# Layer 0 of a two-layer block on one Trainium2 core: the mLSTM's column-group products of a block in one place, and the 64-feature chunk's low-rank and down products in one place

## The chip, the cores and the metric

The kernel runs on one core of one Trainium2 chip. A time is the device time of one execution in microseconds (us). The kernel before takes 770.57 us, the median of 3 runs (769.84 to 771.42). Everything is float32. TensorE is called PE here, VectorE DVE, ScalarE ACT, GpSimd POOL, and SyncE SP.

## The reference, cut to what matters

The input is 4 sequences of 512 tokens with 256 features. Two layers follow each other; each adds an attention-like part and a feed-forward part to the layer-normed input. The change touches two places of layer 0, the mLSTM's sums and the mixture of low-rank experts:

```python
# mLSTM, 8 heads, 16 key and 32 value features per head
C = (q @ k.T / sqrt(16)) * exp(Dmat - m)              # Dmat from the two gates
n = maximum(abs(C.sum(-1, keepdims=True)), exp(-m))
h = (C / n) @ v
# experts: 704 hidden features, 8 experts of rank 16, two of them chosen per token
base_out = (silu(gate_base) * up_base) @ Wd.T
for e in experts:
    h = silu(gate_base + g_lora_e) * (up_base + u_lora_e)
    acc += (h @ Ad_e.T @ Bd_e.T) * 2.0 * weight_e
x = x + mlstm_block(xn) + base_out + acc
```

The kernel computes the mLSTM block by block: 128 positions of all 4 sequences at a time, with a state (a 16x33 matrix per head and sequence) that goes from block to block.

## The kernel before

**Stages.** Layer 0 works through four blocks j of 128 positions x 4 sequences (512 tokens), layer 1 through the same four. In layer 0, `mlstm(j)` is the attention part, `experts(j)` the mixture, `mlp(j)` the second feed-forward part of the attention block; each is a Python generator that issues instructions.

**What sets the order.** Each engine runs its instructions in the order in which they were issued (`InOrder`). That order comes from a planner in the kernel's own Python: `Clock` keeps a guess of when each engine, tile and PSUM bank is free, and `Flow` always steps the generator that can go on first by that guess. `flow.wait(tiles, banks=n)` hands control away until the tiles are ready and n PSUM banks are free; `flow.add(gen, turn=...)` starts another stream, with a lower `turn` going first. So an edit in one place can move the instructions of all others.

**Array shapes.** A matmul whose operand has only 32 output columns or 32 or 64 contraction rows uses a part of PE's 128x128 array, and 4 or 2 of these run side by side. The profile writes the shape of the part as rows*columns. There are five kinds of such groups in layer 0, and everything else is 128*128:

- 32*128: the products `qk` (16 matmuls of 128 columns for each of two head parities) and `h_ps`, what the old state gives;
- 128*32: `hv` (values) and `sums` (denominators), 16 matmuls for each parity, and `st_ps`, the product for the new state, 16 matmuls of 66 columns;
- 128*64: the hidden chunk of 64 features of each half of the tokens ("pair"), up-projections and the two steps of low-rank corrections;
- 64*128: that pair's two products to the experts' ranks (`acc<-he_pair,lora`), and its four down products (`acc<-WdT,hid`, 64 rows).

**mlstm.** After the decays are known, the state's product is a stream of its own (`pass_on`): it transposes the keys to tokens, multiplies them with `wvs` into a PSUM tile `st_ps`, masks that on DVE and adds it to the decayed `state`. Meanwhile the main stream gets the decay matrices `ct[0]` and `ct[1]` (a DMA, a POOL select, a DVE subtraction and an ACT exponential each), multiplies them with `qk`, and then, for each parity s, issues `hv` and `sums` when `ct[s]` is ready.

**experts.** Of 704 hidden features, five chunks have 128 and the last 64. The order of work is the pair of 64-feature chunks, then five chunks of the first half of the tokens, then five of the second; each chunk has a base product and two low-rank steps, between which ACT and DVE read its bank (`gated`). Four turns later, its product to the ranks is added to `dps[half]`, a PSUM accumulator (`acc`). When the first half's five are through, the pair's product for both halves is added: it is the last one of `dps[0]` and the first of `dps[1]`. Then `finish(half, t)` scales `dps[half]` on DVE (`tmp<-acc,tmp`, then `dw<-tmp`), for half 0 at once; for half 1 it also issues the down products into two more accumulators `yps`: four of 64 rows, then for each half ten of `hid` and two of `dw` (`acc<-BdT,dw`), and DVE adds the result to x.

Of the kernel before, what the change touches and what calls it, by code (L numbers as in the profile page):

```python
# [13 lines left out]
P = 128  # L14
# [19 lines left out]
def layers_kernel(ctx: ExitStack, tc: tile.TileContext, io: dict, out: bass.AP):  # L34
# [168 lines left out]
    def mm_ps(name):  # L203
        count[0] += 1
        t = psum.tile([P, 512], F32, tag="mm", bufs=BANKS, name=f"{name}_{count[0]}")
        clock.take_bank(t)
        return t
# [20 lines left out]
    class Flow:  # L228
# [21 lines left out]
        def idle(self, t, why=""):  # L250
            if t > self.now:
                clock.stalls.append((self.now, t - self.now, "idle " + why))
                clock.free["pe"] = t

        def soon(self, us=0.5):
            return self.now + us
# [238 lines left out]
    with ExitStack() as l0:  # L495
# [5 lines left out]
        def tmp():  # L501
            return new(wk0, [P, 512], "tmp", 7)
# [199 lines left out]
        def mlstm(j):  # L702
# [149 lines left out]
            if not last:  # L852
                yield from flow.wait(dec)
                for b in range(B):
                    wvs.append(new(wk0, [P, H, DV + 1], "wv", 4))
                    pool.tensor_tensor(
                        out=wvs[b], in0=va[:, b, :, :], in1=spread_dec(new_n, b), op=ALU.mult)
            faded = set()

            def pass_on():  # L860

                k_tok = new(wk0, [P, B, P], "qs")
                yield from flow.wait(kT, banks=1)
                kt_ps = mm_ps("kt_ps")
                for b in range(B):
                    transpose(kt_ps[:, cols_of(b)], kT[:, cols_of(b)], ident)
                act.copy(k_tok, kt_ps.rearrange("p (b c) -> p b c", c=P))
                yield from flow.wait(*wvs, k_tok, banks=1)
                st_ps = mm_ps("st_ps")
                for b in range(B):  # L870
                    for r in range(H // 2):
                        mine = slice(32 * r, 32 * r + 32)
                        mm(st_ps[mine, b * W2 : (b + 1) * W2], k_tok[:, b, mine],
                           wvs[b][:, 2 * r : 2 * r + 2, :].rearrange("p i d -> p (i d)"),
                           start=True, stop=True, at_once=4)
                new_state = state if first else wvs[0].rearrange("p (b i) d -> p b i d", b=B)
                dve.tensor_tensor(
                    new_state, st_ps[:, 0 : B * W2].rearrange("p (b i d) -> p b i d", b=B, i=2),
                    parity.unsqueeze(1).unsqueeze(3).to_broadcast([P, B, 2, DV + 1]), ALU.mult)
                while not first and not faded:  # L880
                    yield flow.soon()
                if not first:
                    yield from flow.wait(state)
                    yield flow.spare()
                    dve.tensor_tensor(state, state, new_state, ALU.add)
                passed.add(j)

            if not last:
                flow.add(pass_on(), 1)
# [7 lines left out]
            if not first:  # L897
                for b in range(B):
                    mine = hr[:, b, :, :]
                    pool.tensor_tensor(out=mine, in0=mine, in1=spread_dec(old_n, b), op=ALU.mult)  # L900
                    yield flow.soon(0.6)
                if not last:
                    heads = state.rearrange("p b i d -> p (b i) d")
                    pool.tensor_tensor(
                        out=heads, in0=heads, in1=fade.rearrange("p b i -> p (b i)").unsqueeze(
                            2).to_broadcast([P, 2 * B, DV + 1]), op=ALU.mult)
                faded.add(j)
            for s in range(2):
                for r in range(0, H // 2, 2):
                    yield from flow.wait(ct[s])  # L910
# [8 lines left out]


            dve.tensor_copy(ones_at[:, :, DV], rr[:, 0, :])
            sums = None
            hvT = [ct[0][:, 2, :], ct[0][:, 3, :], ct[1][:, 0, 0:P]]

            def by_columns(out, lhsT, s, start, stop):
# [27 lines left out]
            for s in range(2):  # L953
                yield from flow.wait(ct[s], banks=4)
                qks = [mm_ps("qk") for _ in range(H // 2)]
                for b in range(B):
                    for r, qk in enumerate(qks):
                        mm(qk[:, cols_of(b)], kT[32 * r : 32 * r + 32, cols_of(b)],
                           qm[32 * r : 32 * r + 32, s, cols_of(b)], start=True, stop=True,
                           at_once=4)  # L960
                for r, qk in enumerate(qks):
                    dve.tensor_tensor(ct[s][:, r, :], qk, ct[s][:, r, :], ALU.mult)
            for s in range(2):
                yield from flow.wait(ct[s], banks=1 if sums else 2)
                hv = mm_ps("hv")
                by_columns(hv, lambda b, r: va[:, b, 2 * r + s, 0:DV], s, True, True)
                if not sums:
                    sums = mm_ps("sums")
                    clock.held.add(sums.tensor.name)
                by_columns(  # L970
                    sums[:, 0:P], lambda b, r: ones_at[:, b, DV - 2 * b - s : 2 * DV - 2 * b - s], s,
                    s == 0, s == 1)
                act.copy(hvT[s], hv)
                if s == 1:
                    act.copy(hvT[2], sums[:, 0:P])
                    clock.held.discard(sums.tensor.name)
            for n in range(3):
                yield from to_tokens(n)

# [166 lines left out]
        def experts(j):  # L1146
# [60 lines left out]
                while read[n] < 0:  # L1207
                    yield flow.soon(0.2)

            rooms, hb, he, dps = {}, {}, {}, {}  # L1210

            dws, mine = {}, [slice(half * (P // 2), (half + 1) * (P // 2)) for half in range(2)]

# [5 lines left out]
            def released(ps):  # L1219
                clock.held.discard(ps[:].tensor.name)  # L1220

            def finish(half, t):


                yield from flow.wait(dps[half])
                dve.tensor_tensor(t, dps[half], t, ALU.mult)
                dw = dws[half] = new(wk0, [P, T], "dw", 2)
                dve.tensor_tensor(dw, slots(t)[:, 0, :], slots(t)[:, 1, :], ALU.add)
                if half == 0:
                    return  # L1230
                yield from flow.wait(banks=2)
                yps = [acc() for _ in range(2)]

                def down(half, i, a, w, stop=False, **kw):
                    mm(yps[half][:, i * D : (i + 1) * D], a[:, i * P : (i + 1) * P], w, stop=stop,
                       skip_group_check=True, **{"start": False, **kw})

                for i in range(2):  # L1240
                    for half in range(2):
                        down(half, i, hb["pair"][mine[half], :], wdT[mine[half], last, :],
                             start=(i == 0), at_once=2)
                for half in range(2):
                    for i in range(2):
                        yield 0
                        for c in range(last):
                            down(half, i, hb[half, c], wdT[:, c, :])
                    yield from flow.wait(dws[half])
                    for i in range(2):  # L1250
                        down(half, i, dws[half], bdT, stop=(i == 1))
                    xv = xb[:, 2 * half : 2 * half + 2, :].rearrange("p b d -> p (b d)")
                    dve.scalar_tensor_tensor(xv, yps[half], 0.5, xv, ALU.mult, ALU.add)
                    released(yps[half])
                mixed.add(j)
# [23 lines left out]
            for i in range(len(order) + 4):  # L1279
# [33 lines left out]
                n = i - 4  # L1313
                if 0 < n < len(order):
                    _, half, c = order[n][0]
                    if (half, c) == (0, 0):
                        yield from flow.wait(banks=1)
                        dps[0] = acc()
                    yield from unread(n)
                    yield clock.ready(he[n])  # L1320
                    mm(dps[half], adT[:, c, :], he.pop(n), start=((half, c) == (0, 0)),
                       stop=((half, c) == (1, last - 1)))
                    if c < last - 1:
                        continue
                    if half == 0:

                        yield from unread(0)
                        yield from flow.wait(he[0], banks=1)
                        dps[1] = acc()
                        for h in range(2):  # L1330
                            mm(dps[h], adT[mine[h], last, :], he[0][mine[h], :], start=(h == 1),
                               stop=(h == 0), at_once=2)
                    weight = tmp()
                    for s in range(K_TOP):
                        dve.tensor_scalar(
                            slots(weight)[:, s, :], wT[:, here(half)],
                            (-LORA_SCALE, LORA_SCALE)[s], 0.0, ALU.mult, ALU.max)
                    if half == 1:
                        weighed.add(j)
                    released(dps[half])  # L1340
                    flow.add(finish(half, weight), turn=1)

        def main():
            for j in range(NJ):
# [271 lines left out]
```

## Time and profile before

| what | value |
|---|---|
| median of 3 runs | 770.57 us (769.84 to 771.42) |
| the profiled execution | 770.89 us |
| its span, first to last instruction | 769.1 us |
| PE matmuls busy in the span | 762.4 us (99%), 3792 records |
| PE weight loads busy | 518.2 us (67%) |
| DVE / ACT / POOL busy | 466.9 (61%) / 225.1 (29%) / 162.8 us (21%) |
| granted TensorE clock | 1.0 |

The profile's page has one line per group of like instructions, with the number, the mean duration of one and the idle time before it. All instructions of the recorded engines have line L221, the helper that issues them, so a group is told by its tiles: `acc<-he_pair,lora` writes tile `acc` and reads `he_pair` and `lora`. A float32 matmul is two records (passes) of PE; a transpose is one. Records of matmuls overlap, since they are pipelined: what one costs the next is the distance of their starts, not the duration. The timeline view lists merged instructions in order: start, length from the first start to the last end, engine, operation, tiles, array shape, form, number.

### The profile page before, as it was taken

The page shows a single profiled execution, that of the slowest core. Times are in us where ns is not written, and L with a number is a line of the kernel's source. Part 1 is how long each engine was busy: PE and PEld are TensorE (multiplying, and loading weights), DVE is VectorE, ACT ScalarE, POOL GpSimd, SP SyncE. Part 2 cuts the span into 40 slices and gives each one's busy share as a digit, 9 for nine tenths or more (in the row PEclk, how much of TensorE's full clock was granted, in tenths as well). Part 3 has the DMA queues.
Part 4 walks back from the last instruction along what each step waited for, and adds up shares of the span by engine and source line. Part 5 has one row for each costly group of instructions (what it writes and reads, how often), then busy time and mean ns, then how long its engine had stood idle before and what let it go on. Part 6 is the DMA issues. An engine that isn't in the chain of part 4 may idle for free.

```text
span 769.1 us, 9739 instructions
## 1 busy us (share of the span) xinstructions
PE 762.4 (99%) x3792; PEld 518.2 (67%) x3792; DVE 466.9 (61%) x1075; ACT 225.1 (29%) x457; POOL 162.8 (21%) x154
## 2 busy tenths in 40 slices
PE   9999999999999999999999999999999999999998
PEld 6786777766667875865777774747545664664487
DVE  6787576956544987633377635341376965934971
ACT  4334224332313343212133312010444224214300
POOL 6221051232041320240030041000333224013100
PEclk9999999999999999999999999999999999999999
DMA  7930000300000200000031110001000000000001
GB/s 236 291 109 1 2 1 0 97 15 0 2 1 1 111 0 1 2 1 0 1 111 36 75 43 13 1 0 55 0 1 0 1 27 1 0 29 0 1 14 42
DMA packets 18959, 25.44 MB, mean 33 GB/s; under 512 B 2784, under 2 KB 12768, under 8 KB 18912
## 3 DMA queue, kind: packets, MB, share of 16 engines
q1 hardware_dynamic: 17824, 24.53, 9.9%
q8 instruction: 30, 0.49, 0.3%
q10 hardware_dynamic: 1088, 0.28, 0.2%
q14 instruction: 17, 0.14, 0.1%
HBM read 22.65 MB, written 2.16 MB: 32 GB/s over the span
## 4 chain that ended last, share of the span: by engine, by line
PE 91%; DVE 8%; issue 1%; DMA 0%; POOL 0%; ACT 0%; SPq 0%; DVEq 0%; POOLq 0%
PE yp L221 18%; PE chunk L221 16%; PE up L221 14%; PE gp L221 14%; PE acc L221 10%; PE qk_ps L221 4%; PE pt L221 2%; PE vp L221 2%; PE o_ps L221 2%; PE v_ps L221 2%; PE lp L221 2%; DVE sl L221 1%; PE qk L221 1%; PE hv L221 1%; DVE tmp L221 1%; PE q_ps L221 1%
## 5 line engine op out<-in xcount | busy, mean ns | idle before, releaser
L221 PE MATMUL chunk<-low,lora 128*128 128x256 f32 (+1 forms) x384 | 86.3, 384 | 1.3 <-DVE he_pair L221 1.1
L221 ACT ACTIVATE sl<-chunk 128x256 f32<-128x256 f32 x132 | 50.7, 384 | 113.7 <-PE chunk L221 100.9
L221 PE MATMUL chunk<-xnT,wguT 128*128 128x256 f32 (+1 forms) x384 | 83.8, 383 | 0.0
L221 PEld LDWEIGHTS chunk<-xnT,wguT 128*128 128x128 f32 (+1 forms) x384 | 63.7, 181 | 20.5 <-issue 8.9
L221 PEld LDWEIGHTS chunk<-low,lora 128*128 128x128 f32 (+1 forms) x384 | 63.5, 181 | 17.1 <-issue 4.4
L221 DVE SCALAR_TENSOR_TENSOR sl<-sl,chunk 128x256 f32<-128x256 f32 x132 | 54.6, 414 | 23.9 <-ACT sl L221 23.5
L221 PE MATMUL up<-featT,w_up 128*128 128x512 f32 x128 | 60.4, 594 | 0.0
L221 PE MATMUL gp<-featT,w_gate 128*128 128x512 f32 x128 | 60.3, 593 | 0.0
L221 PE MATMUL up<-xnT,lora 128*128 128x512 f32 x128 | 60.2, 592 | 0.0
L221 PE MATMUL gp<-xnT,wguT 128*128 128x512 f32 x128 | 60.2, 592 | 0.0
L221 PE MATMUL yp<-w_down,hid 128*128 128x256 f32 x256 | 56.4, 379 | 0.0
L221 PE MATMUL yp<-w_gate,hs 128*128 128x256 f32 x256 | 56.1, 379 | 0.0
L221 PEld LDWEIGHTS yp<-w_down,hid 128*128 128x128 f32 x256 | 48.5, 190 | 8.2 <-issue 1.9
L221 PEld LDWEIGHTS yp<-w_gate,hs 128*128 128x128 f32 x256 | 48.6, 190 | 6.6
L221 DVE SCALAR_TENSOR_TENSOR tmp<-tmp,gp 128x512 f32<-128x512 f32 x32 | 22.0, 687 | 45.6 <-ACT tmp L221 45.6
L221 ACT ACTIVATE tmp<-gp 128x512 f32<-128x512 f32 x32 | 19.1, 597 | 95.0 <-PE gp L221 95.0
L221 POOL TENSOR_TENSOR pd<-k,q 128x256 f32<-128x256 f32 (+3 forms) x16 | 24.6, 1539 | 97.8 <-ACT k L221 96.5
L221 PEld LDWEIGHTS gp<-xnT,wguT 128*128 128x128 f32 x128 | 24.2, 190 | 28.8 <-issue 28.0
L221 PEld LDWEIGHTS up<-xnT,lora 128*128 128x128 f32 x128 | 24.2, 190 | 28.4 <-issue 27.5
L221 PEld LDWEIGHTS gp<-featT,w_gate 128*128 128x128 f32 x128 | 24.2, 190 | 28.1 <-issue 27.7
L221 PEld LDWEIGHTS up<-featT,w_up 128*128 128x128 f32 x128 | 23.9, 190 | 27.2 <-issue 26.1
L221 PE MATMUL acc<-tmp,lora 128*128 128x512 f32 x80 | 40.8, 598 | 0.0
(221 smaller groups left out, 1188.3 us busy)
## 6 DMA issues: line engine op xcount, KB each, us to landing
ct<-m_dram SPq DMA_DIRECT2D x8, 1024.0 KB, 8.5
x<-in_x SPq DMA_DIRECT2D x3, 512.0 KB, 9.7
out<-x SPq DMA_DIRECT2D x6, 256.0 KB, 2.2
w_gate<-in_w_gate SPq DMA_DIRECT2D x1, 1024.0 KB, 7.0
w_up<-in_w_up SPq DMA_DIRECT2D x1, 1024.0 KB, 7.6
w_down<-in_w_down SPq DMA_DIRECT2D x1, 1024.0 KB, 10.2
wguT<-in_f_gate SPq DMA_DIRECT2D x1, 1024.0 KB, 5.0
lora<-in_f_up SPq DMA_DIRECT2D x1, 1024.0 KB, 4.9
```

The source lines that it names most:

```text
L221: return tc.keep_in_program_order(f(*args, **kw))
```

## The change

It does three things. In `mlstm` the state's 16 products leave `pass_on`, which now only transposes the keys (its result goes into `k_toks`). The main stream waits for both `ct`, the weighted values, the keys and three free banks, and then issues both `hv`, both `sums` and the state's products one behind the other; the state's products go to columns 128 to 391 of the bank of `sums`. Between the groups it lets waiting streams with a negative turn go on (`flow.first`), which issue no matmuls. In `experts` the pair's product to the ranks moves from the middle of the block into `finish`, which is now one stream for both halves: it issues the two rank products and the four 64-row down products one behind the other, and a stream `low_rank` with turn -1 scales both `dps` on DVE after that; the products with `dw` wait for it. Both `dps` accumulators are held until then.

```diff
+        def first(self):
+            for s in [s for s in self.streams if s[2] < 0 and s[0] <= self.now]:
+                self.step(s)
...
                 act.copy(k_tok, kt_ps.rearrange("p (b c) -> p b c", c=P))
-                yield from flow.wait(*wvs, k_tok, banks=1)
-                st_ps = mm_ps("st_ps")
-                for b in range(B):
-                    for r in range(H // 2):
-                        mine = slice(32 * r, 32 * r + 32)
-                        mm(st_ps[mine, b * W2 : (b + 1) * W2], k_tok[:, b, mine],
...
-                passed.add(j)
+                k_toks.append(k_tok)
...
             for s in range(2):
-                yield from flow.wait(ct[s], banks=1 if sums else 2)
-                hv = mm_ps("hv")
-                by_columns(hv, lambda b, r: va[:, b, 2 * r + s, 0:DV], s, True, True)
-                if not sums:
-                    sums = mm_ps("sums")
-                by_columns(
...
+            while not last and not k_toks:
+                yield flow.soon()
+            yield from flow.wait(*ct, *([] if last else [*wvs, *k_toks]), banks=3)
+            hvs = [mm_ps("hv") for _ in range(2)]
+            sums = mm_ps("sums")
+            for s in range(2):
+                flow.first()
+                by_columns(hvs[s], lambda b, r: va[:, b, 2 * r + s, 0:DV], s, True, True)
+                flow.first()
                 by_columns(
                     sums[:, 0:P], lambda b, r: ones_at[:, b, DV - 2 * b - s : 2 * DV - 2 * b - s], s,
                     s == 0, s == 1)
+                act.copy(hvT[s], hvs[s])
+            if not last:
+                st = sums[:, P : P + B * W2]
+                for b in range(B):
+                    for r in range(H // 2):
+                        mine = slice(32 * r, 32 * r + 32)
+                        mm(st[mine, b * W2 : (b + 1) * W2], k_toks[0][:, b, mine],
...
+            act.copy(hvT[2], sums[:, 0:P])
+            if not last:
+                new_state = state if first else wvs[0].rearrange("p (b i) d -> p b i d", b=B)
+                dve.tensor_tensor(
...
+                if not first:
+                    dve.tensor_tensor(state, state, new_state, ALU.add)
+                passed.add(j)
...
-            def finish(half, t):
-                yield from flow.wait(dps[half])
-                dve.tensor_tensor(t, dps[half], t, ALU.mult)
-                dve.tensor_tensor(dw, slots(t)[:, 0, :], slots(t)[:, 1, :], ALU.add)
-                if half == 0:
-                    return
-                yield from flow.wait(banks=2)
+            def finish():
+                yield from unread(0)
+                yield from flow.wait(he[0], banks=2)
                 yps = [acc() for _ in range(2)]
+                for h in range(2):
+                    mm(dps[h], adT[mine[h], last, :], he[0][mine[h], :], start=False, stop=True,
+                       at_once=2, skip_group_check=True)
                 for i in range(2):
                     for half in range(2):
                         down(half, i, hb["pair"][mine[half], :], wdT[mine[half], last, :],
                              start=(i == 0), at_once=2)
+
+                def low_rank():
+                    for half, t in enumerate(weights):
+                        yield from flow.wait(dps[half])
+                        dve.tensor_tensor(t, dps[half], t, ALU.mult)
+                        released(dps[half])
+                        dve.tensor_tensor(dw, slots(t)[:, 0, :], slots(t)[:, 1, :], ALU.add)
+                flow.add(low_rank(), turn=-1)
...
-                    if half == 0:
-                        yield from flow.wait(he[0], banks=1)
-                        dps[1] = acc()
-                        for h in range(2):
-                            mm(dps[h], adT[mine[h], last, :], he[0][mine[h], :], start=(h == 1),
...
-                    flow.add(finish(half, weight), turn=1)
+            weighed.add(j)
+            flow.add(finish(), turn=1)
```

## The prediction

> **What bounds the kernel.** First the page: busy times, slices, and the chain that ended last.
>
> ```profile
> PE 762.4 (99%) x3792; PEld 518.2 (67%) x3792; DVE 466.9 (61%) x1075; ACT 225.1 (29%) x457; POOL 162.8 (21%) x154
> ...
> PEclk9999999999999999999999999999999999999999
> ...
> PE 91%; DVE 8%; issue 1%; DMA 0%; POOL 0%; ACT 0%; SPq 0%; DVEq 0%; POOLq 0%
> ```
>
> PE has work in 99% of the span at the full granted clock, and the chain is PE. So the time is the sum of the distances between starts of PE's records, plus its few waits, and an edit is worth what it does to these two. The number of records stays: the instruction order of the changed program has the same 2012 matmuls and transposes, and as many DVE, ACT and POOL instructions. What can change is what lies between the records, so I read PE's timeline in narrow windows. In the undisturbed stretches a pass of 512, 256 or 128 columns starts 429, 216 or 109 ns after the one before. Around the state's product and the pair's products of block 0 it doesn't:
>
> ```profile
> 36.63 0.38 PE L221 MATMUL chunk<-low,lora 128*128 128x256 f32 x1
> 36.94 0.67 PE L221 MATMUL st_ps<-wv,qs 128*32 128x66 f32 x32
> 37.54 0.70 PE L221 MATMUL chunk<-xnT,wguT 128*128 128x256 f32 x2
> ```
>
> ```profile
> 58.77 0.59 PE L221 MATMUL acc<-tmp,lora 128*128 128x512 f32 x1
> 59.29 1.13 PE L221 MATMUL acc<-he_pair,lora 64*128 64x512 f32 x4
> 60.35 0.92 PE L221 MATMUL chunk<-xnT,wguT 128*128 128x256 f32 x3
> ```
>
> Each change of the array's shape costs. The group starts 0.31 us after a pass that takes 0.216 (36.63 to 36.94), and 0.52 after one that takes 0.429: 0.093 us to go in, the same at all 33 places where no wait adds to it. Of the 0.60 us of the state's group (36.94 to 37.54), eight sets of four passes at 58 ns are 0.46; 0.02 goes to the first set, 0.11 to the way out. The pair's group holds 1.06 us (59.29 to 60.35) for two passes' worth of 0.429: 0.105 to fill, 0.095 to leave. And behind both, the second full pass is late: the two records from 37.54 end at 38.24 and last 0.38 each, so the second starts 0.32 after the first and not 0.216: 0.104 us (0.056 where a transpose follows). A visit to a part-array shape thus costs 0.3 to 0.4 us, whatever it computes.
>
> **The change part by part.**
>
> *The state's products* (blocks 0, 1, 2). Their own visit was 0.093 + 0.60 + 0.104 = 0.80 us (0.75 in block 1, before transposes). Behind `sums`, in the same 128*32 shape, they cost their eight sets, 0.46 us, and 0.01: the trace has no 66-column set behind a 128-column one, but where `hv` gives way to `sums` the period stays 0.11 without a gap. Gain 0.33 + 0.28 + 0.33 = 0.94 us.
>
> *The pair's products* (four blocks). Two visits become one. The rank products' own visit costs 0.093 + 1.06 + 0.104 = 1.26; the four down products hold 1.06 as well (0.105 + 4 x 0.216 + 0.09) and cost 1.26. Together: 0.093 + 0.105 + 2 x 0.429 + 4 x 0.216 + 0.09 + 0.104 = 2.11. Gain 0.40, in block 1 0.35: 1.55 us.
>
> *What stands beside them.* The order shows 15 changes of shape fewer, 59 for 74, and 8 groups fewer, 31 for 39. Block 3's column products came in two visits and come in one, but lose a neighbour of part-array shape: 0.12 us gained. In block 2 the down products lose such a neighbour and the old state's products win one: nothing. Sum of the shapes: 0.94 + 1.55 + 0.12 = **2.6 us**. [...]
>
> *Waits that go.* After the first 19 us, PE waits in layer 0 at five places. Two keep their surroundings in the new order (blocks 0 and 3, near 29 and 386 us). Three don't:
>
> ```profile
> 64.78 1.02 PE L221 MATMUL acc<-tmp,lora 128*128 128x512 f32 x2
> 65.97 1.13 PE L221 MATMUL chunk<-low,lora 128*128 128x256 f32 x4 [0.16 <-DVE hid L221]
> ```
>
> ```profile
> 63.98 0.69 DVE L221 TENSOR_TENSOR tmp<-acc,tmp 128x512 f32<-128x512 f32 x1
> 64.70 0.43 DVE L221 TENSOR_TENSOR dw<-tmp 128x256 f32<-128x256 f32 x1
> 65.04 0.41 DVE L221 SCALAR_TENSOR_TENSOR sl<-sl,chunk 128x256 f32<-128x256 f32 x1
> 65.49 0.42 DVE L221 TENSOR_TENSOR hid<-chunk,sl 128x256 f32<-128x256 f32 x1
> ```
>
> (a) The low-rank step at 65.97 waits for `hid`. Two starts that should be 2 x 0.429 apart (64.78 to 65.97) are 1.19 apart: 0.33 us, and 0.10 for the late pass behind it. DVE was busy with the first half's scaling, 1.06 us from 63.98 to 65.04, which the change takes away from here: gain 0.43.
>
> ```profile
> 181.82 1.47 POOL L221 COPY tmp<-rank 128x512 f32<-128x512 f32 x1 [21.14 <-DVE rank L221]
> ...
> 270.17 2.61 POOL L221 TENSOR_TENSOR hr<-hr,dec 128x264 f32<-128x264 f32 x4
> ```
>
> (b) Near 183 us the `spread` transposes wait 0.24 + 0.06 us for this POOL copy. In the new order they stand behind the two products with `dw`, 4 passes or 0.86 us later: gain 0.29. (c) Near 271 us the transposes of block 3's `xn` wait 0.79 + 0.06 us, since DVE's four normalisations took 2.33 us beside the POOL products shown (1.71 us at 60.19). In the new order POOL computes their `rstd` ahead of its four `wv` products, where it stood behind them and a select: gain 0.85. Together 1.57 us.
>
> *A wait that comes.* In block 1 the pair's second low-rank step now stands two matmuls (four passes of 0.216) behind its first. Before, 8 transposes of 0.109 stood between as well. It needs ACT and DVE to have read the bank. Blocks 0 and 3 had this same neighbourhood already, with one to three short instructions more: there PE lost 0.99 us (28.91 to 30.11) and 0.31 (386.26 to 386.78). Block 0 had DVE's `by_row` work in the way; block 1 has none in the order, so I take a value near block 3's, plus its 0.11 us transpose: 0.42; the ends are 0.31 and 0.99.
>
> *What the moved work hides behind.* The scaling of both halves now runs on DVE (0.69 + 0.43 each, 2.2 us) under ten down products of 2 x 0.216 = 4.3 us: nothing, with 2 us to spare; 1.1 us of that goes when `dw` meets a POOL select, as at 153.95 (1.53 us instead of 0.43). Queued behind a late `dw` on PE would be two `BdT` products and all that follows. The bank of `sums` is read later by the state's 0.46 us; nine transposes wait for it, behind the copies of `hv`: below 0.1. For waits that the new order makes elsewhere, I take 0.5 us, a third of the 1.57 that the old order had unplanned; the ends are 0 and 1.6.
>
> **Sum.** -2.6 - 1.57 + 0.42 + 0.5 = -3.25 us against the profiled execution's 770.89 (span 769.1 and 1.8 around it, which stays): 767.6. The median of the runs shown is 0.32 lower, so **767.3 us**.
>
> **The rivals.**
>
> 1. *The shapes gain, the waits return.* DVE and POOL are as busy as before, and every neighbourhood is new: -2.6 + 0.42 + 1.57 - 1.57 = -2.2, or 768.4. For it: three unplanned waits in the old order. Against: (a) is taken away by the change itself. 0.25.
> 2. [...] What a shape costs beyond its entry returns at the next full pass: 15 x 0.093 = 1.4, and the waits' 0.65, give 768.5. [...] Against it: fill and late pass appear at every visit, and vanish where two part-array groups touch. 0.05.
> 3. *Slower: the block's end waits for DVE.* Both halves' scaling now comes last and PE's `BdT` products need it. It decides from the point where DVE is over 2 us behind when the rank products end. The longest hold-up of a DVE instruction in the trace is 1.7 us (a `ct` subtraction of 2.93 beside a POOL select, 1.22 alone). If DVE were 4 us late in all four blocks, 4 x 2 = 8 us: 770.57 - 3.25 + 8 = 775.3. 0.05.
> 4. *Better:* nothing new waits: -2.6 - 1.57 + 0.31 = -3.9, or 766.7 and below. 0.10.
>
> That the change doesn't do what it says is ruled out by the order.
>
> **How the numbers follow.** Forecast 767.3 with 0.55 (its own range 766.7 to 768.0). The range takes in rivals 1, 2 and most of 4, and the run-to-run spread of 0.8: 766.2 to 769.4. A measurement of this kernel tells about 0.2%, 1.5 us, from no change; faster means below 769.0. That holds for the forecast, rival 4, most of rivals 1 and 2: 0.84; within: 0.12; slower: 0.04.
>
> **What would show it.** In the profile after: no `st_ps` group; 32 passes of 66 columns right behind `sums` at 58 ns a set; one 64*128 group per block, of twelve records and about 1.92 us; no wait near `hid` in block 0; a wait of 0.3 to 1.0 us for `he_pair` at the start of block 1; PE's span shorter by about 3 us, all of it in layer 0, and layer 1 as long as before. It would be wrong if PE's waits for `dw`, `tok` or a bank came to over 1 us.

## The result and the profile after

| | before | after |
|---|---|---|
| median of 6 runs each | 770.80 us | 768.06 us (767.93 to 768.51) |
| ratio, 95% interval | | 0.9966 (0.9955 to 0.9976) |
| span of the profiled execution | 769.1 us | 766.4 us |
| from the first `chunk` matmul to the start of the last matmul | 746.38 us | 743.78 us |
| changes of array shape | 74 | 59 |

The changed kernel is 0.34% faster; 767.3 was predicted, in a range of 766.2 to 769.4. The stretch in the table leaves the start-up out, whose length differs from execution to execution (the first `chunk` matmul starts at 19.23 us before and 19.05 after, where nothing was changed). I use it below where tenths matter; it is read from the profiled execution alone.

The page of after: busy times, and the chain that ended last.

```profile
PE 759.7 (99%) x3792; PEld 520.1 (68%) x3792; DVE 466.7 (61%) x1075; ACT 224.8 (29%) x457; POOL 161.9 (21%) x154
...
PE 94%; DVE 5%; issue 0%; ACT 0%; POOL 0%; DVEq 0%; POOLq 0%
```

PE is busy for 2.7 us less with the same number of records, and a smaller part of the chain runs through DVE. PE's timeline of after around block 0's column products:

```profile
88.59 1.08 PE L221 MATMUL hv<-ct,va 128*32 128x128 f32 x32
...
91.24 1.06 PE L221 MATMUL sums<-ct,ones_at 128*32 128x128 f32 x32
92.11 0.64 PE L221 MATMUL sums<-wv,qs 128*32 128x66 f32 x32
92.69 0.55 PE L221 MATMUL tok<-ident,ct 128*128 128x128 f32 x3
```

The state's set now follows `sums` without a gap, 0.87 us after it, as `sums` follows `hv`. The whole visit holds 4.09 us; block 3's, without a state, holds 3.63. So the state's products cost 0.46 us where they cost 0.80 (0.75 in block 1) before. The pair's rank products and the 64-row down products are one group of twelve records in each block (at 77.83, 171.91, 303.17 and 425.85 us), which holds 1.92 us from its first start to that of the next full pass.

Where PE still waits after the start-up in layer 0, in the waits view of after:

```profile
PE chunk L221 <- DVE he_pair L221: 1.1, 2, 0.9
PE chunk L221 <- DVE ss L221: 0.4, 1, 0.4
PE pt L221 <- DVE xn L221: 0.3, 1, 0.3
```

The first line is the pair's second low-rank step in blocks 0 and 3, as before; the second is the same step of block 1, the wait that was forecast. This view counts the time in which PE is idle; by the distance of starts the three cost 0.99 and 0.31 us as before, and 0.50. The third was not forecast. In the timeline it is in block 3, and one of its kind is in block 2 (a row has the array shape of its first record: the x12 below are eight passes of 128*64 and four of 128*128):

```profile
109.72 2.15 PE L221 MATMUL chunk<-low,lora 128*64 128x256 f32 x12
112.29 1.93 PE L221 MATMUL chunk<-low,lora 128*64 128x256 f32 x11 [0.43 <-DVE ss L221]
...
155.00 1.30 PE L221 MATMUL pt<-ident,xn 128*128 128x128 f32 x8
156.32 1.13 PE L221 MATMUL chunk<-low,lora 128*128 128x256 f32 x4
...
272.45 0.49 PE L221 MATMUL pt<-ident,xn 128*128 128x128 f32 x3
273.29 0.77 PE L221 MATMUL pt<-ident,xn 128*128 128x128 f32 x5 [0.35 <-DVE xn L221]
```

Eight transposes at 0.109 us take 0.87; those from 155.00 take 1.32 to the next matmul, and 0.10 more is lost to the late pass behind them. What DVE and POOL did at these two places:

```profile
153.32 2.16 DVE L221 TENSOR_SCALAR xn<-x,mv,rstd 128x256 f32<-128x256 f32 x4
...
152.49 2.52 POOL L221 TENSOR_TENSOR wv<-va,dec 128x264 f32<-128x264 f32 x4 [1.58 <-ACT dec L221]
...
270.14 3.10 DVE L221 TENSOR_SCALAR xn<-x,mv,rstd 128x256 f32<-128x256 f32 x4
...
270.11 1.12 POOL L221 TENSOR_TENSOR rr<-rr,mhalf 128x4 f32<-128x4 f32 x1
271.08 4.02 POOL L221 TENSOR_SCALAR_AFFINE_SELECT ct<-ct 128x2048 f32<-128x2048 f32 x2
```

In the kernel before, four that nothing held up took 0.40 us each:

```profile
151.95 1.37 DVE L221 TENSOR_SCALAR xn<-x,mv,rstd 128x256 f32<-128x256 f32 x4
```

Here they take 2.16 and 3.10 us beside POOL's instructions. (The 1.71 us at 60.19, which the prediction compares with and an expectation below calls undisturbed, has POOL's `w_out` beside it, from 59.27 to 61.11, and two of its four took 0.56 and 0.58.) In block 3 the first three are through in 1.05 us; the fourth begins with the first of the two selects (271.08 to 273.09) and ends at 273.24, 0.15 behind it.

### The profile page after: what moved, and what is told of

Same layout as the page of the kernel before. It is cut to its first block, busy times and chain, and to the rows that moved or that the text cites. A ratio compares the mean times of both kernels' runs of the same rounds, so it can differ in the third digit from the quotient of the medians.

```text
span 766.4 us, 9748 instructions
## 1 busy us (share of the span) xinstructions
PE 759.7 (99%) x3792; PEld 520.1 (68%) x3792; DVE 466.7 (61%) x1075; ACT 224.8 (29%) x457; POOL 161.9 (21%) x154
## 3 DMA queue, kind: packets, MB, share of 16 engines
HBM read 22.65 MB, written 2.16 MB: 32 GB/s over the span
## 4 chain that ended last, share of the span: by engine, by line
PE 94%; DVE 5%; issue 0%; ACT 0%; POOL 0%; DVEq 0%; POOLq 0%
PE yp L221 18%; PE chunk L221 17%; PE up L221 14%; PE gp L221 14%; PE acc L221 11%; PE qk_ps L221 4%; PE pt L221 2%; PE vp L221 2%; PE o_ps L221 2%; PE v_ps L221 2%; PE lp L221 2%; PE qk L221 1%; PE sums L221 1%; PE hv L221 1%; PE q_ps L221 1%; DVE sl L221 1%
## 5 line engine op out<-in xcount | busy, mean ns | idle before, releaser
L221 POOL TENSOR_TENSOR ss<-ss,mhalf 128x32 f32<-128x32 f32 x4 | 22.0, 5500 | 101.0 <-DVE ss L221 101.0
```

The lines of the kernel that those rows point to most:

```text
L221: return tc.keep_in_program_order(f(*args, **kw))
```

## The experiments

All times are medians, ratios are against the kernel before on the same chip, and the last column is the stretch from the first `chunk` matmul to the start of the last one, in the profiled execution. A kernel whose edit keeps the planner's guesses (its instructions are issued without `clock.issue`, or with the old one's cost) has the same order on the other engines.

| kernel | median us | ratio, 95% interval | stretch us |
|---|---|---|---|
| before | 770.80 to 771.05 | | 746.38 |
| after | 768.06 | 0.9966 (0.9955 to 0.9976) | 743.78 |
| mlstm_part | 769.45 | 0.9985 (0.9976 to 0.9994) | 745.52 |
| experts_part | 773.25 | 1.0029 (1.0018 to 1.0040) | 750.25 |
| cut_in_three | 771.48 | 1.0009 (1.0000 to 1.0018) | 746.95 |
| dw_late | 769.61 | 0.9983 (0.9974 to 0.9992) | 745.19 |
| norm_on_act | 768.38 | 0.9966 (0.9954 to 0.9978) | 743.88 |
| experts_part_norm_on_act | 771.84 | 1.0016 (1.0005 to 1.0027) | 748.50 |
| experts_part_offset_on_pool | 768.77 | 0.9968 (0.9956 to 0.9981) | 744.40 |
| base_between | 765.92 | 0.9934 (0.9922 to 0.9946) | 741.62 |
| base_between_norm_on_act | 767.41 | 0.9952 (0.9939 to 0.9965) | 742.48 |
| base_between_half_on_act | 765.66 | 0.9929 (0.9917 to 0.9942) | 741.17 |
| four_behind | 771.74 | 1.0006 (0.9997 to 1.0015) | 747.29 |
| four_between | 776.72 | 1.0070 (1.0057 to 1.0083) | 752.02 |

### What a visit to a shape costs

**cut_in_three** puts one full down product ahead of the 64-row ones and one in their middle:

```diff
                 for i in range(2):
+                    down(0, i, hb[0, 0], wdT[:, 0, :], start=(i == 0), plan=False)
                     for half in range(2):
                         down(half, i, hb["pair"][mine[half], :], wdT[mine[half], last, :],
-                             start=(i == 0), at_once=2)
+                             start=(i == 0 and half == 1), at_once=2)
...
-                            down(half, i, hb[half, c], wdT[:, c, :])
+                            down(half, i, hb[half, c], wdT[:, c, :], emit=(half, c) != (0, 0))
```

> The changed kernel, with the group of twelve 64*128 records cut in three in each block: one of the full-array down products that follow is put ahead of the four 64-row products, one in their middle. The same 2012 matmuls and transposes, the same order on every other engine, and 8 more visits to a part-array shape (75 changes of shape for 59). Theory (a visit costs entry 0.093, fill 0.105, way out 0.09 and a late second pass 0.104): 8 x 0.39 = 3.1 us slower than the changed kernel, that is 0.4 us above before. [...] Rival (the shapes are worth nothing, the change gained by its new order): within 0.3 us of the changed kernel.

Measured: 3.17 us more than after in the stretch, 0.40 for each of the 8 visits. The waits are after's within 0.1 us. The way in alone, 0.093 at each of 16 changes of shape (1.5), and the order alone (0.3) are ruled out: it is the visit that costs, with all four of its parts.

**four_behind and four_between** test the same for the column products. Both add matmuls into unused columns of the bank of `sums`. four_between calls `extra` behind each `hv` and each `sums` (in block 3 not behind the last), four_behind as often in the loop shown, ahead of the copy of `sums`:

```diff
+            def extra():
+                pe.matmul(sums[:, 392:512], ident, ident[:, 0:120], start=True, stop=True,
+                          skip_group_check=True)
...
+            for _ in range(3 if last else 4):
+                extra()
```

> The changed kernel with 15 further full-array matmuls of 120 columns that nobody reads (four in blocks 0 to 2, three in block 3), all of them directly behind the column products of a block, in the same order otherwise. This is the base for the next kernel. Two passes of some 0.103 us each: 15 x 0.206 = 3.1 us, a span of 769.5. All theories expect the same.

> The same 15 full-array matmuls, now one behind each of hv, sums, hv and sums of a block (three in block 3), so that the column products come in five visits (four in block 3) instead of one: 15 more visits, 30 more changes of shape. Theory (a visit of this shape costs entry 0.093, first set 0.02, way out 0.11 and a late second pass of 0.056 to 0.104): 15 x 0.28 to 0.33 = 4.2 to 4.9 us more than with the four behind. [...] Rival (a visit costs nothing by itself): the same span.

The timeline of four_behind, then that of four_between:

```profile
91.17 1.06 PE L221 MATMUL sums<-ct,ones_at 128*32 128x128 f32 x32
92.05 0.64 PE L221 MATMUL sums<-wv,qs 128*32 128x66 f32 x32
92.62 1.15 PE L221 MATMUL sums<-ident 128*128 128x120 f32 x8
```

```profile
89.03 1.08 PE L221 MATMUL hv<-ct,va 128*32 128x128 f32 x32
90.04 0.48 PE L221 MATMUL sums<-ident 128*128 128x120 f32 x2
90.45 1.08 PE L221 MATMUL sums<-ct,ones_at 128*32 128x128 f32 x32
```

Measured: four_behind 3.5 us above after (3.1 was expected; the passes of 120 columns follow each other by 0.112 us and not 0.103), and four_between 4.73 us above that in the stretch, 0.315 for a visit: in the 4.2 to 4.9 of the theory, where the way in alone, 0.093 at each of 30 changes, would come to 2.8. In the spans the difference is 5.2, since four_between's start-up was 0.5 us longer. From 89.03 to 90.45 a set of 16 and an extra matmul take 1.42 us; in four_behind such a set takes 0.88 (91.17 to 92.05), and the four extra matmuls together 0.99.

### The two parts by themselves

**mlstm_part** is the kernel before with the diff's `first` and `mlstm`; **experts_part** is the one with the diff's `experts` alone.

> The mLSTM's part of the change alone: the state's products behind the sums; the pair's rank products stay in the middle of the block. The order of this kernel has 68 changes of shape, against 74 before and 59 with the whole change. Theory (each visit to a part-array shape costs 0.3 to 0.4 us, and what a new order makes PE wait comes on top): the three state groups give 0.94 us; but block 0's down products of 64 rows, which had the column products for a neighbour, now stand alone, and the pair's products of blocks 0 and 2 lose the state's group beside them, so that about 0.8 us of shapes is left. The waits: block 1 gets the same neighbourhood of its two low-rank steps as with the whole change, 0.5 us; the waits near 183 and 271 us are in other surroundings and may go (0.3 and 0.85). Together 0.8 to 1.6 us below before. [...] Rival (the gain of the whole change is the new order's waits and not the shapes): shapes give nothing, the time stays within 0.5 us of before.

Measured: 0.86 us less in the stretch (1.3 in the span, since the start-up was 0.46 shorter). Block 1's pair waits 0.50 for its second step, as expected; the waits at 65.97, 183 and 271 are gone, and a new one of 0.63 us near 162 takes back most of the last. The entries, holds and late passes of all its part-array visits come to 0.85 us less than before, where about 0.8 was expected.

> The experts' part of the change alone: the pair's rank products directly ahead of the four 64-row down products; the state's products stay a stream of their own. The order has 69 changes of shape, against 74 before and 59 with the whole change, since hv and sums of blocks 1 and 2, which came in one visit, now come in two. Theory: the four merged groups give 1.55 us, the two more visits of the column products take 0.6 back, neighbours give 0.3: shapes 1.3 us below before. The waits: the one near 65.97 (0.43) should go, since DVE's scaling of the first half has left that place; the one of block 3's normalised tokens stays. Together 1.3 to 2 us below before. [...] If the two parts were independent, this run and that of the mLSTM's part would add up to the 2.7 us of the whole change; by the order they fall short by about 0.6 us, since each part makes neighbours of the other.

This missed: the part alone is 3.9 us slower in the stretch than before. That is the profiled execution, the slowest of seven (771.80 to 774.52); by the medians the part is 2.45 us slower. It isn't the shapes: 64*128 groups of twelve records hold 1.92 us here too, and all part-array visits together come to 0.99 us less than before (1.3 was expected). The whole change has 2.64 less, 0.80 more than the two parts together: it leaves 28 visits of 35, the parts 33 and 32, since each makes neighbours for the other. It isn't `dw` either, for which PE never waits. Two places make it. PE's transposes of `xn` wait 1.40 us near 155, with 0.35 behind, and near 271 the timeline shows this:

```profile
271.24 1.02 PE L221 MATMUL acc<-tmp,lora 128*128 128x512 f32 x2
272.95 0.30 PE L221 MATMUL pt<-ident,xn 128*128 128x128 f32 x1 [0.68 <-DVE xn L221]
...
274.78 0.77 PE L221 MATMUL pt<-ident,xn 128*128 128x128 f32 x5 [0.31 <-DVE xn L221]
275.38 3.58 PE L221 MATMUL chunk<-xnT,wguT 128*128 128x256 f32 x8
...
270.77 3.96 DVE L221 TENSOR_SCALAR xn<-x,mv,rstd 128x256 f32<-128x256 f32 x4
...
270.65 2.01 POOL L221 TENSOR_SCALAR_AFFINE_SELECT ct<-ct 128x2048 f32<-128x2048 f32 x1
272.62 2.60 POOL L221 TENSOR_TENSOR hr<-hr,dec 128x264 f32<-128x264 f32 x4
```

The four normalisations take 3.96 us, until POOL is nearly through; PE waits 0.85, 0.44, 0.53 and 0.53 us for them one after the other. And then eight passes of 256 columns take 3.38 us from 275.38 to the next form at 278.76, where they take 1.73 elsewhere. The windows view of the same kernel says why (busy time and number for PE, PEld, DVE, ACT and POOL, then the granted clock):

```profile
274.50:279.00 4.50, 4.22 (x14) 3.49 (x15) 2.80 (x11) 1.07 (x3) 1.31 (x3) 0.62 0.00 0
```

So the place costs twice in this execution: 2.4 us of waits, and 1.65 us of passes at half the clock. The wait (c) of the prediction, here in other surroundings, grew from 0.85 to 4. The half clock doesn't come in every execution: a core's mean clock was 0.998 in two of the seven runs, this one among them, and 1.0 in five, which still took 771.80 to 773.53 us.

**experts_part_norm_on_act** takes the normalisations off DVE.

```diff
+        if ms is not None:
+            off = new(pool, [P, B], "off", 2)
+            dve.emit("scalar_tensor_tensor", off, mv[:, :, 0], -1.0, rstd, ALU.mult, ALU.mult)
         for b in range(B):
+            if ms is not None:
+                ops = (xn[:, b, :], x[:, b, :], mv[:, b, 0:1], rstd[:, b : b + 1])
+                clock.issue("dve", "tensor_scalar", ops, {})
+                act.emit("activation", xn[:, b, :], x[:, b, :], AF.Identity,
+                         bias=off[:, b : b + 1], scale=rstd[:, b : b + 1])
+                continue
```

> The experts' part alone, with the same normalisations on ACT; the order on PE and POOL as in the experts' part. There the normalisations took 4.56 us for three beside a POOL select near 152 and 3.96 us for four near 271 (1.71 for four undisturbed); PE waited 1.75 and 2.41 us, and behind the second of these its passes took twice the time for 3.4 us (granted clock 0.62 from 274.5 to 279), 1.65 us more. Theory (it was this that made the part slower than before, and the shapes gained what they should): 5.8 us less, a span of 767.0, 1.3 to 2.3 us below before's 769.1. Rival (the part is slower by itself, through the longer way to dw or the split columns): a span of 771 or more. If the halved clock came from PE's waits, it is gone with them; if it has another cause, the span is 768.6.

Half of it came: the span is 771.1, in the rival's range, with the waits near 155 gone (1.75 us). The ones near 271 are there still, 1.34 us and three of 0.38, and five passes of 256 columns at half the clock (0.50 granted from 273.50 to 276.50). The single small instruction that the edit left on DVE is the reason. The view of tile `off` (shortest, median and longest in ns), and the timeline:

```profile
L216 DVE SCALAR_TENSOR_TENSOR off<-mv,rstd x3: 151/155/1906, 59.0 to 269.2; 128x4 f32<-128x4 f32 x3
```

```profile
269.07 2.02 POOL L224 TENSOR_SCALAR_AFFINE_SELECT ct<-ct 128x2048 f32<-128x2048 f32 x1
...
271.13 2.08 ACT L216 ACTIVATE xn<-x,off,rstd 128x256 f32<-128x256 f32 x4 [2.69 <-DVE off L216]
...
271.79 0.33 PE L224 MATMUL pt<-ident,xn 128*128 128x128 f32 x1 [1.18 <-ACT xn L216]
```

Four numbers in each partition take 0.15 us twice, and 1.91 us the third time: from 269.19, just behind the start of a POOL select, to 271.10, when the select ends at 271.09. Not every POOL instruction did this, as far as the profile's spans of POOL, which are rough, can tell: in block 2 the same DVE instruction ran inside POOL's `rr` and took its 0.15 us.

```profile
151.11 1.00 POOL L224 TENSOR_TENSOR rr<-rr,mhalf 128x4 f32<-128x4 f32 x1
...
151.56 0.15 DVE L216 SCALAR_TENSOR_TENSOR off<-mv,rstd 128x4 f32<-128x4 f32 x1
```

**experts_part_offset_on_pool** lets POOL make that offset, behind `rstd` and ahead of the select:

```diff
+        if ms is not None:
+            off = new(pool, [P, B], "off", 2)
+            dve.emit("tensor_scalar", off, mv[:, :, 0], -1.0, None, ALU.mult)
...
         inv_sqrt(rstd, rstd)
+        if ms is not None:
+            pool_e.emit("tensor_tensor", out=off, in0=off, in1=rstd, op=ALU.mult)
```

> The experts' part alone with the normalisations on ACT, and the offset of four numbers a token row made by POOL directly behind rstd, not by DVE. With DVE that offset (128x4) had taken 1.91 us beside a POOL select and PE had waited 1.34 us and four times 0.38 for it, with passes of twice the time behind (1.1 us). Theory (what made the experts' part slow is DVE held up by POOL): these waits and the halved passes go too, 771.1 less 3.7, a span of 767.2 to 767.7, some 1.6 us below before's 769.1. Rival (the part is slow by itself, or the halved clock has another cause than PE's waits): 769 or more.

```profile
268.26 0.20 POOL L216 TENSOR_TENSOR off<-off,rstd 128x4 f32<-128x4 f32 x1
...
268.50 2.08 ACT L216 ACTIVATE xn<-x,off,rstd 128x256 f32<-128x256 f32 x4
...
270.43 1.04 PE L224 MATMUL pt<-ident,xn 128*128 128x128 f32 x8
271.31 1.89 PE L224 MATMUL chunk<-xnT,wguT 128*128 128x256 f32 x8
```

The waits and the slow passes are both gone: a span of 767.0, a little below the theory's range, and 1.98 us less than before in the stretch. That settles the larger question: the experts' part gains what it should (1.3 to 2 was expected), and what made it slow alone was DVE held up by POOL. That the halved clock came from PE's waits fits, since none of the five runs has a mean clock of 0.998; but with two of seven and five of twelve in the two kernels that have the waits, five runs are few. The hold-up itself is still there: the DVE instruction that is left for `off`, a `tensor_scalar` on four numbers with one tile as input, took 1.88 us from 264.94 beside a select from 264.78 to 266.79. It stands early enough that PE didn't wait for it.

### The waits that were left

**norm_on_act** is the first of these edits in the changed kernel.

> The changed kernel, with the four normalisations of xn of blocks 1, 2 and 3 on ACT instead of DVE (a scale and an offset for each token; one small DVE instruction makes the offset); the same order on PE and POOL, and on DVE but for these. Theory (DVE's normalisations are held up by POOL's instructions that run at the time, and PE's two waits for xn and for the hid behind it in blocks 2 and 3 come from that): these waits go, 0.55 us near 155 and 0.57 near 272; a span of 765.3 to 765.6 instead of 766.4, that is 1.0 us less, or 0.2 less than that if block 1's transposes near 57 now wait for ACT. Rival (the normalisations are late because rstd is late, not because of DVE): the two waits stay, within 0.2 us of 766.4.

```profile
154.38 2.08 ACT L216 ACTIVATE xn<-x,off,rstd 128x256 f32<-128x256 f32 x4 [1.37 <-DVE off L216]
...
156.51 0.77 PE L224 MATMUL pt<-ident,xn 128*128 128x128 f32 x5 [0.16 <-ACT xn L216]
```

It missed: 0.1 us more than after. Block 3's wait is gone (0.57), but block 2's has the same size with another owner (0.09 and 0.38 for ACT, which takes 0.49 us from one normalisation to the next), and block 1's transposes, which had not waited, now wait 0.16 and 0.38. One engine's pace was no better than the other's hold-up.

**dw_late** asks how much the moved scaling has to spare:

```diff
                         dw = dws[half] = new(wk0, [P, T], "dw", 2)
+                        for _ in range(0 if half else 8):
+                            tc.keep_in_program_order(nc.vector.tensor_tensor(
+                                dw, slots(t)[:, 0, :], slots(t)[:, 1, :], ALU.add))
```

> The changed kernel, with eight more DVE instructions in each block that write the first half's dw before the one that counts (0.35 us each from start to start), in the same order otherwise: dw of the first half is 2.8 us later in each block. By the prediction's account (2 us to spare) PE then waits 0.8 us for dw in each block, with the late pass behind it 0.9: 3.6 us slower than the changed kernel. By the trace after, dw lay ready 3.7, 4.0, 4.0 and 4.7 us before its product: no wait for dw, and what DVE does later for others (its readings of the chunks, the rank of the router) costs between 0 and 1.5 us.

```profile
81.55 3.65 DVE L1252 TENSOR_TENSOR dw<-tmp 128x256 f32<-128x256 f32 x8
85.23 0.42 DVE L221 TENSOR_TENSOR dw<-tmp 128x256 f32<-128x256 f32 x1
...
85.71 1.13 PE L221 MATMUL acc<-BdT,dw 128*128 128x256 f32 x4
...
185.84 0.66 PE L221 MATMUL spread<-ident,tmp 128*128 128x128 f32 x4 [1.16 <-POOL tmp L221]
```

The eight took 0.46 us each, not 0.35, so that `dw` was 3.68 us late (81.55 to 85.23). PE waited for it 0.05 us in block 0, where 3.7 were to spare, and not at all in the others. Of the 1.41 us that were lost, 1.38 are one wait near 184 us: the router's ranks, queued behind on DVE, reached POOL's copy and the `spread` transposes late. A late DVE hurt here first through what is queued behind.

**base_between** gives PE work for the pair's wait:

```diff
+                    while (step == 2 and len(rooms) < min(i + AHEAD, len(order))
+                           and clock.room(1) <= flow.now
+                           and (read[n] < 0 or clock.over(rooms[n]) > flow.now)):
+                        yield from base(len(rooms))
                     yield from unread(n)
```

> The changed kernel, where experts may issue one further chunk's base product (8 passes, 1.7 us) between a chunk's two low-rank steps if a bank is free and the second step would have to wait for the readers of its bank. The order has 60 changes of shape for 59. Theory (the waits of 0.99, 0.50 and 0.31 us ahead of the pair's second step in blocks 0, 1 and 3 are PE's lack of other work while ACT and DVE read the bank): all three go, 1.8 us, and a change of shape adds 0.1: a span of 764.5 to 765.0 for 766.4. Rival (a wait only moves, since the chunk's readings on DVE come in the same total): at least half of it is found again at a later chunk, 765.5 or above.

```profile
107.27 2.14 PE L221 MATMUL chunk<-low,lora 128*64 128x256 f32 x12
109.25 1.89 PE L221 MATMUL chunk<-xnT,wguT 128*128 128x256 f32 x8
111.07 3.22 PE L221 MATMUL chunk<-low,lora 128*64 128x256 f32 x17
```

All three waits are gone and none came back: 2.16 us less than after in the stretch and a span of 764.4, 0.1 below the theory's range. These waits are 1.8 of it, and block 3's wait for `xn` went with the new order too.

**base_between_norm_on_act** and **base_between_half_on_act** add the normalisations on ACT, all four, or two there and two on DVE with the offset by POOL (the condition is `ms is not None and b % 2`).

> Both of these: the base product between the pair's steps, and the normalisations on ACT. If the waits are separate they add up: 1.7 and 1.0 us below the changed kernel, a span of 763.6 to 764.2. If the normalisations' waits depend on which POOL instruction runs beside them, they may have gone already in the new order of the first of the two, and then ACT brings nothing or 0.3 us back (its normalisations come in front of the chunks' tanh, which DVE needs): 764.5 to 765.2.

> The version with a base product between the pair's steps, and of the four normalisations of xn two on DVE and two on ACT side by side, the offset made by POOL. There DVE's four took 2.17 us near 152, and PE waited 0.16 for xn and 0.18 for the hid behind it, with 0.06 and 0.10 of late passes. On ACT one takes 0.49 us, so two on each engine are through in 1.0 to 1.3 us. Theory: the wait goes, 0.4 us less, a span of 763.9 to 764.1 for 764.4. Rival (ACT's tanh and copies come later behind them, or POOL's products behind the offset): no gain, 764.3 or above.

All four on ACT: 0.86 us more in the stretch than base_between (765.7 in the span, with a start-up 0.45 us longer), outside both ranges: besides ACT's pace in block 2 (0.47) PE waits 0.25 and 0.25 near 63, for `hid` and `tmp`, with late passes behind. Two and two: 0.45 less in the stretch, a span of 763.7, below the theory's range. The timeline of the latter:

```profile
150.95 1.08 ACT L216 ACTIVATE xn<-x,off,rstd 128x256 f32<-128x256 f32 x2
...
151.95 1.20 DVE L224 TENSOR_SCALAR xn<-x,mv,rstd 128x256 f32<-128x256 f32 x2
...
153.58 1.04 PE L224 MATMUL pt<-ident,xn 128*128 128x128 f32 x8
```

At 765.66 us (ratio 0.9929) it is the best version of the study, ahead of both kernels; against base_between alone the runs (765.80 to 766.07 there, 765.44 to 765.92 here) overlap.

## Why the prediction was right

By its own steps, in us:

| step | predicted | measured |
|---|---|---|
| state's products | -0.94 | -0.96 (0.46 left of 0.80, 0.75, 0.80) |
| pair's products, groups of 1.92 | -1.55 | -1.54 (1.92 in all four blocks) |
| neighbours | -0.12 | -0.14 (block 3's column products) |
| (a) wait for `hid` at 65.97 | -0.43 | -0.43 |
| (b) wait of `spread` near 183 | -0.29 | -0.29 |
| (c) transposes of block 3's `xn` | -0.85 | -0.28 |
| pair's second step in block 1 | +0.42 | +0.50 |
| waits elsewhere | +0.5 | +0.55 (block 2's `xn` and the `hid` behind it) |
| start-up | 0 | -0.18 |
| sum | -3.25 | -2.77; the two spans, 769.14 and 766.36, differ by 2.78 |

- *The shapes* are right to 0.03 us (2.64 for 2.61), and cut_in_three and four_between show that it is the visit that is paid. Rival 2, in which only the way in at each change counts, is out: 0.40 and 0.315 us were paid for a visit, against 0.19 for its two changes at 0.093. What lies behind the 0.093 no run shows.
- *Wait (c)* is the step that failed. The prediction named the mechanism, normalisations on DVE beside POOL, but concluded that it would go because POOL makes `rstd` ahead of the `wv` products. It does, and yet not earlier (266.76 us after, 266.24 before), and DVE was not waiting for it: the normalisations stood behind its readings of the chunks and began at 270.14 us after, 269.95 before. Beside them now ran a select, and the four took 3.10 us instead of 2.33. 0.57 of the 0.85 were left. With the 0.55 in block 2 this mechanism cost 1.1 us. The profiled execution was to take 767.6 and took 768.07, and (c) is more than the whole difference. That the median of 768.06 is nearer to rival 1 (768.4) than to the centre of 767.3 has a second reason: the centre is 0.3 lower because of the median of before that was shown, 770.57, and the six runs have 770.80. Rival 1's reason, that all of the 1.57 returns, did not hold, since (a) and (b) stayed away.
- *Waits elsewhere*: the 0.5 was a third of another sum, with no place named. That 0.55 came is luck in the size; what came is the mechanism of (c) once more, at a place that the prediction did not look at.
- *The wait that comes* was 0.50 against 0.42. Its cover, the eight transposes, is gone as said, and base_between shows that any other matmuls serve.
- *The moved scaling* costs nothing, as predicted, but its margin was mis-sized: not 2 us but 3.7 to 4.7 from the end of the first half's `dw` to its product, because only that half's 1.1 us stand ahead of it, and the four 64-row products (0.96 us in block 1) run while DVE works, ahead of the ten.
- *Rival 3* (slower, because of DVE) didn't occur in the changed kernel by its own path. experts_part shows that a slower outcome was near by another: half of the change, in an order with selects beside the normalisations, is 2.45 us slower by the medians and 3.9 in the profiled execution. What decided was the order that the planner made of the whole change, not the shapes. With that in view, a chance of 0.04 for slower looks too small.
- Of the signs that were listed: no `st_ps` group, the state's set right behind `sums`, twelve records in 1.92 us, no wait near `hid` in block 0, 0.50 at the start of block 1 and no wait for `dw`, `tok` or a bank are all there; the span is 2.8 us shorter for about 3, and layer 1's one wait is 0.24 us, as before.

## What to carry to other kernels

Where PE bounds the kernel, count the visits to part-array shapes and not the matmuls in them: here each cost 0.3 to 0.4 us, and products of one shape that stand next to each other paid it once (the state's cost 0.46 us there and 0.80 by themselves). Before a change of order is believed, look for the DVE instructions that feed PE and lie beside a long POOL instruction, here a select of 2.0 us, in the new order, since a few such meetings can cost more than the change brings: experts_part was 3.9 us slower in the stretch, with 0.99 us less for its shapes. Where PE waits for ACT and DVE to read a bank (0.99, 0.50 and 0.31 us here), put independent matmuls there; in the stretch that gained 2.16 us, where the whole change gained 2.60.

## What the runs showed of the hardware that was not expected

- In experts_part_norm_on_act a DVE instruction on four numbers in each partition took 1.91 us instead of 0.15, until a POOL select ended. Its end went by when POOL was through and not by its size: in after a normalisation of 256 columns, 0.40 us alone, took 2.14 beside a select and ended 0.15 us behind it. Not every DVE instruction was held up: beside the select of before from 268.19 to 270.20 the readings of `chunk` took 0.41 and 0.42, as elsewhere. And which POOL instruction it is mattered: beside `rr` of 1.0 to 1.1 us the instruction on four numbers took 0.15 and a normalisation 0.40, and beside the `wv` and `hr` products a normalisation took up to 0.73.
- Waits of PE that are short one by one can be followed by half the clock: in experts_part, behind 0.85, 0.44, 0.53 and 0.53 us within 3.1 us, the mean granted clock was 0.62 in the 4.5 us from 274.50, which is 3.4 us at half; in experts_part_norm_on_act it was 0.50 from 273.50 to 276.50 and 0.95 in the 4.5 us ahead of that, about 3.4 us again; while one wait of 1.40 us in a piece, near 155 in experts_part, was not followed by it. What decides it no run here shows, nor why a mean clock of 0.998, which 3.4 us at half the clock make of 770, stands in only two of the seven runs of experts_part and five of the twelve of experts_part_norm_on_act. The latter spread over 769.92 to 774.97 us in 12 runs, and experts_part_offset_on_pool, without the waits, over 768.59 to 768.87; but the seven runs of the former with a clock of 1.0 spread over 769.92 to 771.95 too, so the clock is not all of it.
- The way in at a change of shape is not the larger part of its price: of 0.40 us for a visit of 64*128, 0.093 is the way in and 0.09 the way out; the late second set (0.105) and the late second full pass (0.104) are the rest.
